# A residual kernel with a generated right-hand matrix: first chunks of W and base loaded singly, base chunk 0 cast ahead of W chunk 1, one product of zeros for five, two base units moved up

## The chip, the cores and the metric

The kernel runs on one core of one Trainium2 chip. A core has five engines, each with its own queue of instructions: TensorE (PE in the profile; its weight loads are PEld), VectorE (DVE), ScalarE (ACT), GpSimd (POOL) and SyncE (SP, which here only issues transfers). The metric is the device time of one execution in microseconds; lower is better.

## The reference

x has 8 batches of 1024 rows of 512. A second input, cond (8 x 512), makes for each batch a 512 x 512 matrix of rank 8, which is added to a fixed matrix `base`. Then each batch gets a second, modulated product with a fixed matrix W. Cut to what matters:

```python
ae = layernorm(cond, ln_g, ln_b)                       # 8 x 512
h = gelu(ae @ w1 + b1)                                 # 8 x 512
xw = h @ w2 + b2                                       # 8 x 8192, w2 is 16 MB
x_a, x_b = split(xw, 2); each reshaped to (8, 512, 8)
layer = base[None] + einsum('bdr,bkr->bdk', x_a, x_b)  # 8 x 512 x 512
x = x + (x + einsum('btc,bco->bto', x, layer))
ys = cond * 512 ** -0.5
d = rsqrt((ys * ys) @ (W * W) + 1e-8)                  # 8 x 512
x = x + einsum('bsi,io->bso', x * ys[:, None], W) * d[:, None]
```

## The kernel before

All matrices are held in four chunks of 128 rows (k = 0 to 3), one after the other along the free dimension of a tile of 128 partitions. For each batch b the kernel makes one matrix, P_b = (2I + base + rank term) · (I + diag(ys_b) W diag(d_b)), so that the output is one product per batch, x_b · P_b. Every product of 32-bit floats is done as three products of `fp32r` tiles: each operand is split into a head (rounded; names with h) and a rest (names with l), and head·head, head·rest and rest·head are added up in PSUM. One such triple of 128 x 128 by 128 x 512 products, for one chunk k and one block c of output rows, is called a base unit when its left operand is base.

The program first sets up (to about 80 us) and then runs the main loop over 8 batches and 8 row tiles (`po`, line 799), in which TensorE is the only limit. In the setup almost everything is in an order written out by hand (`InOrder`, `keep_in_program_order`): each engine runs its instructions in the order of the program's text.

The setup's steps that the change and the prediction touch, with the names of the profile:

- **Loads** (lines 86 to 92), all issued by SP in this order: `sm` (small vectors, identity), `cnd` (in tile `scr`), W chunks 0 and 1 (`w_sb`), base chunks 0 and 1 (`b_raw`), W chunks 2 and 3, base chunks 2 and 3, then `w1` (the page calls it `w_sb<-in_w` too), then the sixteen 1 MB tiles of `w2` (`w`) as buffers come free, with `consts`, `condrows`, `b2rows` and `base` between them.
- **Zeros** (lines 102 to 111): twelve products of a tile of zeros (`warm`), started at once, and five more (`keep_warm(5)`, line 256) between the transposes `pa` of the normalised cond (`ae`) and the first base products. Their results are not used.
- **Right operands of the first batch**: `round_yw(k)` (ScalarE, W chunk times ys, head `nh`), `rest_yw(k)` (VectorE, rest `nl`). d is not known yet and is multiplied in later.
- **Left operands**: `twice_i(k)` (VectorE, adds 2I to the diagonal block), `round_b(k)` (ScalarE, head `bh`; for chunk 0, VectorE does the first 128 columns and ScalarE the other 384), `rest_b(k)` (VectorE, rest `bl`).
- **First base products** (`pg`, line 257): all four head·head products of chunk 0, then the four head·rest (`nl`), then the four rest·head (`bl`). Then chunk 1 (`first_base`), mixed with the row products for d (`pq_v`, which reads the squares of W, `wsq`) and for h (`pq_z`, which reads `w1`).
- **`w2` groups** (`w2_group`, line 387): each issues the load of a `w2` tile into one of nine big buffers and runs that tile's four products (`px`, eight instructions in the profile). `Fill.units(n)` puts n base units of batches 1 to 3 (`pq`) between them. `rank_t` is a chain of steps on xw's second half: `by`, its transposes `pb`, the product `pt_t`, and the stacked rows `ps_t`; each `next(steps)` runs one step.

The part of lines 725 to 742 that orders this:

```python
w2_group()
w2_group()
fill.units(6)
w2_group()
steps = rank_t()
next(steps)          # by
w2_group()
next(steps)          # its rest
fill.units(4)
w2_group()
next(steps)          # pb, byT
w2_group()
fill.units(2)
fill.round(2, 1)
next(steps)          # pt_t
```

Of the kernel before, what the change touches and what calls it, by code (L numbers as in the profile page):

```python
# [14 lines left out]
P = 128  # L15
NB = 8
NT = 1024
D = 512
# [12 lines left out]
def cond_resid_kernel(ctx: ExitStack, tc: tile.TileContext, small, cond, condrows, consts,  # L31
# [12 lines left out]
    def mm(*args, **kw):  # L44
        tc.keep_in_program_order(nc.tensor.matmul(*args, **kw))  # L45

    def turn(*args):
        tc.keep_in_program_order(nc.tensor.transpose(*args))
# [36 lines left out]
    cnd, ae, xab, drow = scr[:NB, 0, :], scr[:NB, 1, :], scr[:, 2, :], scr[:, 3, :]  # L85
    sy.dma_start(sm, small)
    sy.dma_start(cnd, cond)
    for at in (slice(0, 2), slice(2, 4)):
        sy.dma_start(w_sb[:, at, :], weight[:, at, :])
        sy.dma_start(b_raw[:, at, :], baseT[:, at, :])  # L90
    w1_sb = big_tile("w1_sb")
# [14 lines left out]
    def keep_warm(count):  # L106
        for _ in range(count):
            mm(warm.rearrange("p (a c) -> p a c", c=P), zero,
               zero.unsqueeze(1).to_broadcast([P, D // P, P]), start=True, stop=True)
# [29 lines left out]
    def round_yw(k):  # L139

        se.mul(n0[k][0], w_sb[:, k, :], ysT[:, k, 0:1])
# [6 lines left out]
    def twice_i(k):  # L148
        blk = b_raw[:, k, k * P:(k + 1) * P]
        ve.scalar_tensor_tensor(blk, ident, 2.0, blk, ALU.mult, ALU.add)  # L150

    def round_b(k, lo=0, hi=D, by=se.copy):
        (by(bh[:, k, lo:hi], b_raw[:, k, lo:hi]))
# [29 lines left out]
    rstd = sp.tile([NB, 1], F32, name="rstd")  # L183
    ve.tensor_mul(rstd, r, t)
    ve.tensor_scalar(ae, cnd, mv[:, 0:1], rstd, ALU.subtract, ALU.mult)
    round_yw(1)
    twice_i(0)
    round_b(0, 0, P, ve.tensor_copy)
    round_b(0, P, D)
    twice_i(1)  # L190
    round_b(1)
    rest_yw(0)
# [60 lines left out]
    pa = misc.tile([P, KC, NB], F32, tag="misc", name="pa")  # L253
    for k in range(KC):
        turn(pa[:, k, :], ae[:, k * P:(k + 1) * P], ident[:NB, :NB])
    keep_warm(5)
    for i, (s, m) in enumerate(((bh, n0[0][0]), (bh, n0[0][1]), (bl, n0[0][0]))):
        for c in range(KC):
            mm(pg[c], s[:, 0, c * P:(c + 1) * P], m, start=(i == 0), stop=False)
# [127 lines left out]
    def w2_group():  # L387
        h, r, k = todo.pop(0)
        t = big_tile(f"w2_{h}_{r}_{k}")
        sy.dma_start(t, w2[h, r, k])  # L390
        if len(todo) == 15:
            sy.dma_start(cst, consts)
        if len(todo) == 8:
            sy.dma_start(crow, condrows)
            sy.dma_start(b2r, b2rows)
        if len(todo) == 6:
            b_nat.append(big_tile("b_nat"))
            sy.dma_start(b_nat[0], base)
        for j in range(4):
            mm(px[h][32 * j:32 * j + 32, :], hT[:, k, r, :], t[:, j, :],  # L400
               start=(r == 0 and k == 0), stop=(r == 1 and k == KC - 1))
# [296 lines left out]
    fill = Fill()  # L698
# [31 lines left out]
    next(steps)  # L730
    w2_group()
    next(steps)
    fill.units(4)
    w2_group()
    next(steps)
    w2_group()
    fill.units(2)
    fill.round(2, 1)
    next(steps)
    fill.finish(2, 1)  # L740
# [191 lines left out]
```

## Time and profile before

| | |
|---|---|
| median of 3 runs | 305.32 us (305.03 to 305.65) |
| the profiled execution | 305.47 us, span of its instructions 303.7 us |
| granted TensorE clock, mean | 0.998 |
| TensorE busy | 298.0 us (98% of the span) |
| VectorE / ScalarE busy | 176.4 / 145.9 us |
| read from HBM, written | 40.35 MB, 16.79 MB |

Times in the profile's views are microseconds from the span's start. A line of a timeline gives start, duration, engine, source line, operation, tile written <- tiles read, shapes, and how often; in brackets stands the engine's idle time just before it and what ended that. The source line is often that of a helper (L45 is `mm`, L62 the in-order wrapper), so instructions are told apart by their tiles. A line of the chain of waits gives start, duration and what the end of the program was then waiting on.

### The profile page before, as it was taken

The numbers are of one execution on the slowest core, as the hardware profiler recorded it, in microseconds if no ns is written. First come the engines' busy times: TensorE is split into PE (matmuls) and PEld (weight loads), VectorE is DVE, ScalarE is ACT, GpSimd is POOL, SyncE is SP. The second block draws the span as 40 slices with busy tenths as digits, with TensorE's granted clock in tenths as the row PEclk, the third lists the DMA queues.
The fourth block names the chain that finished last, engine by engine and source line by source line (L and its number), as shares of the span: only waits on it lengthen the run. The fifth ranks groups of instructions, "written<-read, shape, count | busy, mean of one in ns | idle before, by whom it ended". The sixth has DMA issues, their size and how long they took to land.

```text
span 303.7 us, 3551 instructions
## 1 busy us (share of the span) xinstructions
PE 298.0 (98%) x1369; PEld 227.9 (75%) x1369; DVE 176.4 (58%) x262; ACT 145.9 (48%) x212; POOL 5.2 (2%) x14
## 2 busy tenths in 40 slices
PE   8999999999999999999999999999999999999995
PEld 3655565466888888888888888888888888888884
DVE  4779830979678479977456478981266543600000
ACT  4756132256476564355664454743645546621221
POOL 0011000001000000100000000000000000000000
PEclk9999999999999999999999999999999999999999
DMA  6999999642319636631651134354151545322222
GB/s 204 409 427 419 410 421 419 220 188 69 138 69 343 242 124 226 228 120 69 207 193 52 69 108 171 97 162 192 69 207 69 190 178 212 148 106 104 96 76 105
DMA packets 15952, 57.37 MB, mean 189 GB/s; under 512 B 1840, under 2 KB 2352, under 8 KB 11584
## 3 DMA queue, kind: packets, MB, share of 16 engines
q1 hardware_dynamic: 6064, 38.78, 34.5%
q10 hardware_dynamic: 9360, 16.78, 14.7%
q0 software_dynamic: 512, 1.59, 1.6%
q8 instruction: 10, 0.16, 0.2%
q14 instruction: 6, 0.05, 0.1%
HBM read 40.35 MB, written 16.79 MB: 188 GB/s over the span
## 4 chain that ended last, share of the span: by engine, by line
PE 88%; DVE 5%; DMA 4%; ACT 2%; issue 0%; ACTq 0%
PE po L45 57%; PE pp L45 13%; PE pq L45 7%; DMA w<-in_w 4%; PE px L45 3%; PE warm L45 2%; PE pg L45 2%; DVE n L62 2%; PE pr L45 2%; PE pt_t L45 1%; ACT work L62 1%; DVE scr L62 0%; PE ps_t L45 0%; DVE q L62 0%; PE pq_v L45 0%
## 5 line engine op out<-in xcount | busy, mean ns | idle before, releaser
L45 PE MATMUL po<-ph,xs 128*128 128x512 f32 (+1 forms) x520 | 164.2, 386 | 0.0
L45 PEld LDWEIGHTS po<-ph,xs 128*128 128x128 f32 x520 | 97.1, 188 | 19.8
L45 PE MATMUL po<-pl,xs 128*128 128x512 f32 (+1 forms) x260 | 100.3, 386 | 0.0
L62 ACT COPY o<-po 128x512 f32<-128x512 f32 (+1 forms) x65 | 37.8, 581 | 87.0 <-PE po L45 86.8
L45 PEld LDWEIGHTS po<-pl,xs 128*128 128x128 f32 x260 | 48.8, 188 | 9.9
L62 DVE TENSOR_TENSOR xs<-x,xs 128x1024 fp32r<-128x1024 f32 x32 | 38.7, 1221 | 20.5 <-ACT xs L62 20.5
L62 ACT CAST xs<-x 128x1024 fp32r<-128x1024 f32 x32 | 33.0, 1050 | 4.0 <-DMA x<-in_x 2.3
L62 DVE TENSOR_TENSOR nl_p<-n,nh_p 128x1024 fp32r<-128x1024 f32 x14 | 17.1, 1220 | 20.0 <-ACT nh_p L62 20.0
L62 DVE TENSOR_TENSOR pl<-q,ph 128x1024 fp32r<-128x1024 f32 x16 | 19.4, 1220 | 7.3 <-ACT ph L62 7.3
L62 DVE TENSOR_TENSOR q<-pr,q 128x512 f32<-128x512 f32 x24 | 15.8, 685 | 7.9 <-PE pr L45 7.8
L45 PE MATMUL pq<-nh,bh 128*128 128x512 f32 x48 | 19.8, 412 | 0.0
L45 PE MATMUL pq<-nl,bh 128*128 128x512 f32 x48 | 19.1, 398 | 0.1
L45 PE MATMUL pq<-nh,bl 128*128 128x512 f32 x48 | 19.0, 395 | 0.0
L62 ACT CAST ph<-q 128x1024 fp32r<-128x1024 f32 x16 | 16.6, 1051 | 3.9 <-DVE q L62 3.7
L62 DVE SCALAR_TENSOR_TENSOR n<-w_sb,ysT,d 128x512 f32<-128x512 f32 x24 | 17.8, 745 | 0.8 <-DMA d<-d_out 0.8
L62 ACT COPY q<-pp 128x512 f32<-128x512 f32 x20 | 11.7, 587 | 13.3 <-PE pp L45 13.3
L45 PE MATMUL px<-w,hT 128*32 128x512 f32 x128 | 16.0, 601 | 0.4 <-DMA w<-in_w 0.4
L62 ACT CAST nh_p<-n 128x1024 fp32r<-128x1024 f32 x14 | 14.7, 1052 | 2.5 <-PE pp L45 2.4
L45 PEld LDWEIGHTS pq<-nh,bh 128*128 128x128 f32 x48 | 9.0, 188 | 8.4 <-issue 5.0
L45 PE MATMUL pp<-nh_p,sh 128*128 128x512 f32 x32 | 12.4, 389 | 0.0
L45 PE MATMUL pp<-nl_p,sh 128*128 128x512 f32 x32 | 12.4, 389 | 0.0
L45 PE MATMUL pp<-nh_p,sl 128*128 128x512 f32 x32 | 12.4, 389 | 0.0
(135 smaller groups left out, 272.9 us busy)
## 6 DMA issues: line engine op xcount, KB each, us to landing
w<-in_w SPq DMA_DIRECT2D x16, 1024.0 KB, 11.1
x<-in_x SPq DMA_DIRECT2D x16, 1024.0 KB, 5.2
out<-o ACTq DMA_DIRECT2D x63, 256.0 KB, 2.0
d<-d_out POOLq DMA_DIRECT2D x6, 256.0 KB, 3.9
w_sb<-in_weight SPq DMA_DIRECT2D x2, 512.0 KB, 5.4
b_raw<-in_baseT SPq DMA_DIRECT2D x2, 512.0 KB, 6.2
w_sb<-in_w SPq DMA_DIRECT2D x1, 1024.0 KB, 9.6
b_nat<-in_base SPq DMA_DIRECT2D x1, 1024.0 KB, 9.5
```

The costliest lines, as they stand in the source:

```text
L45: tc.keep_in_program_order(nc.tensor.matmul(*args, **kw))
L62: return lambda *a, **kw: pin(f(*a, **kw)) if InOrder.on else f(*a, **kw)
```

## The change

It changes four places. The first four chunk loads become W chunk 0, base chunk 0, W chunk 1, base chunk 1, of 256 KB each; chunks 2 and 3 stay together. In ScalarE's order `round_b(0)` (its 384 columns) changes places with `round_yw(1)`. After `pa` one product of zeros runs instead of five. Two base units that stood after the second `w2` group behind `fill.units(4)` now run before both groups.

```diff
-    for at in (slice(0, 2), slice(2, 4)):
+    for at in (slice(0, 1), slice(1, 2), slice(2, 4)):
         sy.dma_start(w_sb[:, at, :], weight[:, at, :])
         sy.dma_start(b_raw[:, at, :], baseT[:, at, :])
...
-    round_yw(1)
+    round_b(0, P, D)
     twice_i(0)
     round_b(0, 0, P, ve.tensor_copy)
-    round_b(0, P, D)
+    round_yw(1)
     twice_i(1)
     round_b(1)
     rest_yw(0)
...
-    keep_warm(5)
+    keep_warm(1)
...
     next(steps)
-    fill.units(4)
+    fill.units(6)
     w2_group()
     next(steps)
     w2_group()
-    fill.units(2)
     fill.round(2, 1)
     next(steps)
```

## The prediction

> **What bounds the kernel now.** I read the page first (engine shares, the DMA row), then the chain of waits in order of time, the timeline of the first ten microseconds, the DMA view of the first 16, and TensorE's timeline around the one wait for a `w2` tile.
>
> ```profile
> PE 298.0 (98%) x1369; PEld 227.9 (75%) x1369; DVE 176.4 (58%) x262; ACT 145.9 (48%) x212; POOL 5.2 (2%) x14
> ...
> DMA  6999999642319636631651134354151545322222
> ```
>
> TensorE runs its products in program order and is busy almost throughout, so time can only come from the places where it waits or does idle work. The DMA row says that for the first 50 us or so (slices of 7.6 us) the transfer engines are full as well: there, a `w2` tile lands when the bytes ahead of it have passed. The chain of waits shows both:
>
> ```profile
> 0.99 5.00 PE warm L45 x12
> 5.99 0.34 PE pa L48 x4
> 6.33 1.19 PE warm L45 x5
> 7.51 4.38 PE pg L45 x18
> ...
> 34.91 1.90 PE px L45 x16
> 36.81 0.02 issue
> 36.83 11.16 DMA w<-in_w
> 47.99 0.04 issue
> 48.03 1.06 PE px L45 x8
> ```
>
> Two places, then: nothing useful runs on TensorE before 7.5, and at 48.03 it has stood waiting for a tile that landed at 36.83 + 11.16 = 47.99. The front in the timeline (start, duration, engine; all engines):
>
> ```profile
> 5.45 1.33 ACT L62 ACTIVATE nh<-w_sb,ysT 128x512 fp32r<-128x512 f32 x2 [1.44 <-DMA w_sb<-in_weight]
> 6.78 0.29 DVE L62 SCALAR_TENSOR_TENSOR b_raw<-sm,b_raw 128x128 f32<-128x128 f32 x1 [1.30 <-DMA b_raw<-in_baseT]
> 7.10 0.23 DVE L62 CAST bh<-b_raw 128x128 fp32r<-128x128 f32 x1
> 7.25 0.28 DVE L62 SCALAR_TENSOR_TENSOR b_raw<-sm,b_raw 128x128 f32<-128x128 f32 x1
> 7.44 0.76 PEld L45 LDWEIGHTS pg<-nh,bh 128*128 128x128 f32 x4 [0.42 <-ACT bh L62]
> 7.45 0.74 DVE L62 SCALAR_TENSOR_TENSOR nl<-w_sb,ysT,nh 128x512 fp32r<-128x512 f32 x1
> ```
>
> The first base product waits for `bh` chunk 0, that for base's first half, which landed at 6.75. VectorE's `twice_i(1)` (7.25) and then `nl` chunk 0 (7.45) follow at once only because chunk 1 came in the same transfer.
>
> **The change, part by part.**
>
> *Four loads of 256 KB for two of 512 KB.* The loads pass in turn through full engines; the DMA view, in slices of 0.4 us, gives the rate:
>
> ```profile
> GB/s 0 0 0 0 124 138 123 195 317 195 184 297 451 410 420 369 246 215 195 277 328 338 471 410 471 440 430 410 430 471 410 389 492 369 393 441 426 382 448 451
> ```
>
> From 2.4 the slices to 4.8 add up to 525 KB, W's first half at some 230 GB/s; the next three hold base's first half at 427 GB/s; then 521 KB to 8.0, W's second half at 260. W is read slowly, base fast, both with rows of the same size. By bytes, W chunk 0 (first quarter) has passed at 3.7, base chunk 0 at 4.8, W chunk 1 at 5.4, base chunk 1 at 6.0. Before, the half that passed at 4.8 landed at 5.42 and that of 6.0 at 6.75. So the chunks land at about 4.4, 5.4, 6.1 and 6.75. Rows of 2 KB instead of 4 KB cost a little: the 256 KB of `condrows`, with 2 KB rows, landed 0.66 after the load ahead of it, while 256 KB of a 1 MB load take 2.50 / 4 = 0.62; four such pieces add 0.15. Base chunk 1: 6.9; everything behind it, 0.15 later. Two more issues on SP cost 0.35 to 0.43 each, and push W's rest, `w1` and the first `w2` loads back by 0.85; W's rest is then issued at about 3.4 and wanted at 6.2, `w1` at 4.4 and wanted at 9.7, so SP stays ahead. Base's half landed 1.33 after W's, all of it bytes at 512 KB and 427 GB/s, so what a load costs besides its bytes is hidden behind the load ahead of it, and I charge nothing for the two more loads themselves. A rule of the Trainium skill speaks against this part: "DMA: Bandwidth & Descriptors", Anatomy of one DMA, gives each DMA a fixed 2.0 us besides its bytes (a fit for loads issued from GpSimd). If that were paid in turn, two more loads would cost 4 us, base chunk 1 would land at 10.75, and the sum below would end near 308.3; I go by the row.
>
> *Base chunk 0 cast ahead of W chunk 1.* ScalarE: `nh` 0 from 4.4 to 5.1, then its 384 columns of `bh` 0 (0.51) from 5.45 to 5.95. Behind it in the queue `nh` 1 (0.71) waits for W chunk 1, 6.1 to 6.8; its first reader, the products of chunk 1, comes after 9.7. With the old order, `nh` 1 would hold `bh` 0 up to 6.8, so the move is needed. VectorE ends `ae` at 5.47, then `twice_i(0)` and its 128 columns by 6.02 (before: 0.55 from landing to 7.33).
>
> *One product of zeros for five.* Four at 0.23 are 0.92 of TensorE. They were cover: the fifth began at 7.14, and the first base product at 7.47. Now `pa` ends at 6.3, one product ends at about 6.5, and the first base product starts at 6.55, 0.92 earlier; `bh` 0 is ready 0.4 before that. Where the cover is gone, a later chunk costs 1:1.
>
> *What is late next.* The four `nh`·`bh` products take until 7.55 (before 7.47 to 8.47: 1.00). The next need `nl` 0, and VectorE reaches that only after `twice_i(1)`, which now waits for base chunk 1 alone; `nl` 0, `bl` 0, `nl` 1, `bl` 1 all stand behind it. Landing 6.9, + 0.03, + 0.20 to the next start, + 0.74, + 0.05 to TensorE: 7.92. So TensorE stands for 0.37 and goes on at 7.92 against 8.47: 0.55 earlier. `bl` 0 ends at 8.5 and is wanted at 8.9. W chunk 2's square still waits for its landing (9.34 + 0.15) and the squares end at 10.7; the product that reads them starts at 11.82 − 0.55 = 11.27. `bh` 2 (11.64 before, + 0.15) is read at 14.6 or later; `w1` (13.06 + 0.15) at 14.3. From 14 to 36 every wait of TensorE (`pd` at 22.05, `nl` at 27.24) hangs on its own earlier products through VectorE and ScalarE and moves along. **0.55** stays. Bounds: with W read as fast as base, chunk 1 lands 0.8 to 1 earlier and TensorE never stops: 0.92. With W's slowness a price per row rather than per byte, the next part but one.
>
> *Two base units moved up.* Around the wait:
>
> ```profile
> 45.95 1.06 PE L45 MATMUL px<-w,hT 128*32 128x512 f32 x8
> 46.95 0.65 PE L48 MATMUL pb<-sm,work 128*128 128x128 f32 x4
> 48.03 1.06 PE L45 MATMUL px<-w,hT 128*32 128x512 f32 x8 [0.43 <-DMA w<-in_w]
> 49.03 0.50 PE L45 MATMUL pq<-nh,bh 128*128 128x512 f32 x1
> ```
>
> Without a wait this group would start 0.20 after the last `pb` (as `pq_z` does after `pt_v`, 14.64 to 14.85), at 47.53: the wait is 0.50. Two units are 6 products of 0.23 = 1.39. They now stand ahead of the group: 47.53 − 0.55 + 1.39 = 48.37, and the tile lands at 47.99 + 0.15 = 48.14. The wait goes whole, **0.50**, with 0.23 to spare; without the move, the 0.55 of the front would be lost at this place. `pt_t` follows the group directly: `pb` starts 1.0 after the group before, `byT` is done 1.28 later (46.95 to 48.23 before), `pt_t` is reached 2.6 after that group's start: 0.3 of slack. The moved units read `nh`/`nl` of base 2, done at 38.7. The later `w2` tiles keep their slack: the last was issued at 57.48, when the group that ended at 57.35 let go of its buffer, and landed 4.8 later, 0.6 before use; that issue moves with TensorE.
>
> Sum: 0.55 + 0.50 = 1.05. The profiled execution took 305.47 (span 303.7 and 1.77 around it), 0.15 above the median and inside the runs' 305.03 to 305.65. 305.47 − 1.05 = 304.4; from the median it would be 304.3.
>
> **The rivals.**
>
> *Only the second half arrives (no change).* Something at the front (the slow W, a semaphore between chunk and cast) eats the 0.55, for example W's excess, 2.3 − 1.2 = 1.1 us per half, counted per row: chunk 1 of base at 8.0, TensorE at 9.0, 0.5 late, and the 0.50 gained back at 48: 305.4. If just half of it is so, 304.9. For: W alone is slow. Against: base has the same rows and isn't, and the 2 KB rows of `condrows` weren't.
>
> *A thin row of W costs what a thick one did (slower).* Place: W chunks 0 and 1 ahead of base chunk 1. Each then takes W's 2.3 for half the bytes: base chunk 1 lands at 6.75 + 2.3 = 9.05, TensorE goes on at 10.07, 1.60 late, with 0.50 back: 306.6. It decides against the change once base chunk 1 lands after 7.95.
>
> *The clock falls where the zeros are gone (slower).* Row: the zero products start 0.43 apart until 5.2 and 0.23 apart after 6.3, so full speed took some 4.6 us of work; falling back would cost 4.6 / 0.43 = 11 products at 0.20 more, 2.1: 306.5. The longest stand that the trace shows at full clock is 0.58 (21.25 to 22.05); mine is 0.37. "TensorE: Matmul & The Clock Gate", Part 1, puts the window of inactivity at about 3.4 us, by which the clock stays.
>
> **How the numbers follow.** Forecast 0.70 (303.9 to 304.7), no change by the first rival 0.20, thin rows 0.07, clock 0.03. About 0.2%, 0.6 us, is what a measurement of this kernel can tell from no change: faster means under 304.7. Of the forecast a little falls short of that, of the first rival a little passes it: 0.71, 0.20, 0.09. The range runs from the front's best, 0.92 + 0.50 off the median, 303.9, to the first rival's 305.4, rounded out by 0.1 below, and leaves the slower rivals out.
>
> **What would show it.** Right: first base product at about 6.5; `nh` 0 at 4.4; a stand of some 0.4 ahead of `pg<-nl,bh`, which starts near 7.9; `pq_v` near 11.3; no DMA wait at 48, `pt_t` near 49.5 instead of 50.53. Wrong: base chunk 1 landing after 7.5; TensorE standing at the squares (`pq_v`) or at the moved group; a spacing of 0.43 after 7.

## The result and the profile after

The changed kernel took 308.55 us (median of 12 executions, 305.55 to 310.98) against 305.29 for the kernel before: 1.0084 times its time, 95% interval 1.0055 to 1.0114 (the ratio leaves out the two longest executions). The forecast was 304.4, range 303.8 to 305.4, so the time lies outside it, on the side of the slower rivals. The executions differ from each other far more than before, and the mean granted TensorE clock goes with the time: 1.0 in two of them (305.6 and 305.8), 0.993 or 0.994 in seven (307.6 to 309.2) and 0.987 in three (309.6 to 311.0). In the 94 executions of the kernel before that were timed beside the experiments it was 0.997 or more, but for one at 0.995.

The profiled execution is one of the two with a whole clock: 305.55, span 303.6. Its page:

```profile
PE 297.1 (98%) x1365; PEld 227.4 (75%) x1365; DVE 176.5 (58%) x262; ACT 145.9 (48%) x212; POOL 5.1 (2%) x14
...
DMA  6999999652319737631651134255151455422222
```

TensorE is 0.9 us less busy (four products of zeros), and the span is the same: where it no longer runs zeros, it waits. The timeline of the front (start, duration, engine; in brackets the idle time before and what ended it):

```profile
5.70 0.29 DVE L62 SCALAR_TENSOR_TENSOR b_raw<-sm,b_raw 128x128 f32<-128x128 f32 x1
6.40 1.17 PE L45 MATMUL pg<-nh,bh 128*128 128x512 f32 x4
8.25 0.29 DVE L62 SCALAR_TENSOR_TENSOR b_raw<-sm,b_raw 128x128 f32<-128x128 f32 x1 [1.99 <-DMA b_raw<-in_baseT]
8.46 0.74 DVE L62 SCALAR_TENSOR_TENSOR nl<-w_sb,ysT,nh 128x512 fp32r<-128x512 f32 x1
9.25 1.20 PE L45 MATMUL pg<-nl,bh 128*128 128x512 f32 x4 [1.69 <-DVE nl L62]
```

The first base product starts at 6.40 (7.47 before). But VectorE, with `nl` 0 queued behind `twice_i(1)`, waits for base chunk 1 until 8.25, and TensorE stands until 9.25, where before it had gone on at 8.47. A stretch in which TensorE has no product to run is called a stand here; counted from the start of one product to the next, less a product's 0.23, this one is 1.85. The chain of waits says the same in two lines:

```profile
2.93 5.29 DMA b_raw<-in_baseT
...
9.25 3.53 PE pg L45 x14
```

Further on, at the place of the old wait for a `w2` tile, TensorE's timeline has none:

```profile
48.12 1.06 PE L45 MATMUL px<-w,hT 128*32 128x512 f32 x8
49.11 0.66 PE L48 MATMUL pb<-sm,work 128*128 128x128 f32 x4
49.70 1.06 PE L45 MATMUL px<-w,hT 128*32 128x512 f32 x8
50.70 0.50 PE L45 MATMUL pt_t<-wh,work 128*128 128x512 f32 x1
```

`pt_t` starts at 50.70 (50.53 before), although `pq_v` started 0.89 later than before (12.71 against 11.82). So in this execution, with a whole clock, all but 0.17 of the late front is paid back by 50.70, and the time is that of before. What makes the median slower is not in this profile.

### The profile page after: what moved, and what is told of

The parts are those of the page before. It is cut to its first block, busy times and chain, and to the rows that moved or that the text cites. A ratio compares the mean times of both kernels' runs of the same rounds, so it can differ in the third digit from the quotient of the medians.

```text
span 303.6 us, 3547 instructions
## 1 busy us (share of the span) xinstructions
PE 297.1 (98%) x1365; PEld 227.4 (75%) x1365; DVE 176.5 (58%) x262; ACT 145.9 (48%) x212; POOL 5.1 (2%) x14
## 4 chain that ended last, share of the span: by engine, by line
PE 89%; DVE 5%; DMA 2%; ACT 2%; SPq 1%; issue 1%; ACTq 0%; DVEq 0%
PE po L45 57%; PE pp L45 13%; PE pq L45 9%; PE px L45 4%; DVE n L62 2%; DMA b_raw<-in_baseT 2%; PE pg L45 2%; PE pr L45 2%; PE pt_t L45 1%; SPq L62 1%; ACT work L62 1%; DVE nl L62 0%; DVE scr L62 0%; PE ps_t L45 0%; DVE q L62 0%
```

## The experiments

Theory A: base chunk 1 lands late, TensorE stands 1.85 us, and the stand makes the clock fall. Theory B: the long executions have still later landings, the clock only follows. Theory C: it is the four missing zeros that close the clock. Each kernel was timed beside the kernel before: `fill_stand`, `loads_back`, `rest_first` and `units_only` beside 29 executions of it (median 305.39), `no_zeros`, `cast_only`, `rest_first_no_units` and `base_rest_first` beside another 29 (305.53), the three `joint` ones beside 23 (305.66), `mixed` beside 13 (305.25). A ratio is that to the kernel before, with its 95% interval.

**fill_stand.** 

> The changed kernel with eight products of zeros put between the four head-head and the four head-rest products of chunk 0, where its profile shows TensorE standing 1.85 us. Theory A (base chunk 1 lands near 8.2, TensorE stands 1.85 us, and in most executions this stand makes the clock fall for one or two windows, which costs 2 to 4 us): with the stand filled, nearly every execution at clock 0.998 to 1.0 and 305.4 to 306.0 us. Theory B (the long executions are long because chunk 1 lands later still, and the clock only follows): still 307 to 310 us with scatter, and clock below 0.995. Theory C (it is the four zeros missing ahead of the first base product that close the clock): as B.

```diff
     for i, (s, m) in enumerate(((bh, n0[0][0]), (bh, n0[0][1]), (bl, n0[0][0]))):
+        if i == 1:
+            keep_warm(8)
```

306.49 (305.70 to 306.73), ratio 1.0031 (1.0019 to 1.0043), all five executions with a clock of 0.998 or more, where the changed kernel had two of twelve. So it is the stand that makes the clock fall, and filling it with idle work takes some 2 us off the changed kernel's median: against B and C. The time was above what A gave (305.4 to 306.0). In the profile base chunk 1 landed at 9.25, and after the eight zeros TensorE still stood 0.8 until `nl` 0 was ready, so the zeros held nothing up; `pt_t` started at 51.78, 1.25 later than before. So the remaining 1.1 over before goes, in this profile at least, with the late landing itself.

**no_zeros.** 

> The changed kernel without the last product of zeros, so that TensorE idles 0.2 us more ahead of the first base product. One look at the profile. Theory A (stands close the clock in most executions): with chance 0.8 the granted clock falls to half after the stand near 7.5 to 9, products there 0.43 apart instead of 0.23 for one window; 307 to 311 us, mean clock 0.994 or 0.987. Theory B: the clock is whole and the time long all the same.

```diff
-    keep_warm(1)
+    keep_warm(0)
```

One execution, 307.79, clock 0.994: its profile holds the fallen clock. TensorE's timeline, then two views by stretch (start:end, length, busy us of PE, PEld, DVE, ACT, POOL; then the granted clock, the DMA share and GB/s), of this kernel and of the changed one:

```profile
7.02 1.17 PE L45 MATMUL pg<-nh,bh 128*128 128x512 f32 x4 [1.00 <-DVE bh L62]
10.08 1.27 PE L45 MATMUL pg<-nl,bh 128*128 128x512 f32 x4 [1.89 <-DVE nl L62]
11.14 1.91 PE L45 MATMUL pg<-nh,bl 128*128 128x512 f32 x4
```

```profile
7.60:11.00 3.40, 1.51 (x7) 0.94 (x6) 1.93 (x4) 1.73 (x5) 0.00 (x0) 1.00 1.01 363
11.10:14.40 3.30, 3.30 (x9) 2.58 (x8) 3.27 (x10) 2.87 (x5) 0.00 (x0) 0.50 0.99 419
14.50:17.90 3.40, 3.40 (x21) 1.87 (x19) 0.45 (x1) 1.11 (x2) 0.74 (x2) 1.00 1.01 421
```

```profile
5.00:8.40 3.40, 2.57 (x13) 1.19 (x10) 1.26 (x5) 1.91 (x3) 0.00 (x0) 1.00 1.02 306
8.40:11.80 3.40, 2.55 (x11) 2.11 (x12) 3.37 (x9) 3.23 (x6) 0.00 (x0) 1.00 1.03 423
```

The trace's clock record has full speed from 4.22 to 11.05, half from 11.05 to 14.46, full again after: steps of 3.41 us. Four products of `nh`·`bl` take 1.91 instead of 1.10. In the step before the fall TensorE was busy for 1.51 of 3.4. In the changed kernel's profile the steps begin at 5.00 and 8.41, and the stand of 7.40 to 9.25 is cut in two by one: 2.57 and 2.55 of 3.4 busy, and the clock stays. One fallen step costs half of 3.4, 1.7 us, and makes a mean clock of 0.994; two would make 0.989 (one execution of `joint_thin` has that). The 0.987 of three executions of the changed kernel would be two such steps and a piece of one behind the last product, as in the profile before, whose 0.998 comes from half speed after 302.50; no profile holds such an execution. Where the steps lie differs between executions (the first full-speed step began at 3.64 to 6.92 in the profiles). That this is why the same kernel falls in one execution and not in the next is likely, but no pair of profiles of one kernel shows it.

**loads_back.** 

> The changed kernel with the first loads as two of 512 KB again; cast order, one product of zeros and moved units stay. TensorE is then without work from about 6.5 to 7.5 (1.0 us) where the zeros were, and goes on as before the change; the moved units save the 0.5 us wait. Theory A: the thin loads are the cause; chunk 1 lands at 6.75, the stand is 1.0 instead of 1.85 us; about 305.0 us, clock mostly whole. Theory C: without the four zeros the clock falls in most executions, 307 to 309 us. If the clock falls in part of the executions, the length of the stand decides the share.

```diff
-    for at in (slice(0, 1), slice(1, 2), slice(2, 4)):
+    for at in (slice(0, 2), slice(2, 4)):
```

305.14 (304.92 to 306.62), ratio 1.0002 (0.9990 to 1.0015); clock 0.994 in 2 of 11. Base's first half landed at 6.82 and TensorE stood 1.35 ahead of the first base product. As A has it: with the old loads no late chunk and few falls; against C, which had most executions falling. With the zeros gone the stand ahead of the first base product is still long enough for a fall now and then.

**rest_first.** 

> The changed kernel with VectorE's rest of W and of base, chunk 0, ahead of its step that waits for base chunk 1. Theory A: TensorE goes through the twelve products of chunk 0 from 6.4 to about 9.2 without a stand, chunk 1 is ready at about 9.2 to 9.4, the first product that waits is that of the squares (about 11.3 against 11.82 before); 304.4 to 305.0 us, clock at 0.998 or more in nearly all executions, scatter under 1 us. Theory B: gains the stand too, but executions of 307 us and more stay where chunk 1 lands late. Theory C: clock still falls, 306 to 309 us.

```diff
-    twice_i(1)
-    round_b(1)
     rest_yw(0)
     rest_b(0)
+    twice_i(1)
+    round_b(1)
     rest_yw(1)
```

305.01 (304.17 to 306.93), clock 0.998 or more in all 12, ratio 0.9998 (0.9982 to 1.0014). The stand after the first four products is gone, and with it the falls. The scatter stays, against the forecast of under 1 us: two executions took 306.50 and 306.93 with clocks of 1.0 and 0.998. Chunk 1 still lands late (8.26 in this profile), which is the likely reason; no profile of a long execution shows it.

```profile
6.99 1.18 PE L45 MATMUL pg<-nh,bh 128*128 128x512 f32 x4 [0.43 <-DVE bh L62]
8.01 1.10 PE L45 MATMUL pg<-nl,bh 128*128 128x512 f32 x4
8.94 1.08 PE L45 MATMUL pg<-nh,bl 128*128 128x512 f32 x4
```

**units_only.** 

> The kernel before with only the two base units moved up. The wait of 0.5 us at 48.03 goes: 304.8 us, clock 0.998. If what the move gives is taken back later: 305.3 us.

```diff
-    fill.units(4)
+    fill.units(6)
     w2_group()
     next(steps)
     w2_group()
-    fill.units(2)
```

305.37, ratio 1.0000 (0.9990 to 1.0011): no gain; the 304.8 missed. In its profile base's first half landed at 7.30 and the first base product started at 8.02, so the front was 0.55 later than in the profile that the sum was made from. TensorE did not wait at 48, and `pt_t` started at 50.51 (50.53 before): what the move gave, the front had lost.

**cast_only.** 

> The kernel before with ScalarE's cast of base chunk 0 ahead of its step on W chunk 1, nothing else. Both chunks of W and of base come in one load each there, the cast waits for base in either order, and the step on W chunk 1 has 2 us to spare: 305.4 us, as before. Its profile also shows once more when base's first half lands (6.75 in the profile before, 7.30 in that of units_only) and whether TensorE waits near 48.

```diff
-    round_yw(1)
+    round_b(0, P, D)
     twice_i(0)
     round_b(0, 0, P, ve.tensor_copy)
-    round_b(0, P, D)
+    round_yw(1)
```

305.38, ratio 1.0003 (0.9994 to 1.0012), as expected. Base's first half landed at 7.13, the first base product started 0.39 later than in the profile before, and at 48 TensorE did not wait at all: the tile had landed at 47.75.

```profile
47.29 0.65 PE L48 MATMUL pb<-sm,work 128*128 128x128 f32 x4
47.87 1.06 PE L45 MATMUL px<-w,hT 128*32 128x512 f32 x8
```

The two units are in their old place here. So the wait of 0.50 is there in one profile with the old order and not in the other.

**rest_first_no_units.** 

> The changed kernel with chunk 0's rests ahead of VectorE's wait for base chunk 1 (as in rest_first), but the two base units back in their old place. Theory: an early front and the moved units give one gain, not two: without the move, TensorE waits at the second w2 group for the tile that lands near 48, whatever the front gained; median 305.3 to 305.7 us, no execution below 304.8, where rest_first had 305.0 and reached 304.2. Rival: the move is worth nothing by itself even then; 305.0 us as rest_first.

 The edit is rest_first's with the two base units in their old place.

305.49 (305.07 to 307.25), ratio 1.0003 (0.9988 to 1.0018), and no execution below 305.07, where rest_first reached 304.17. In its profile the group waits some 0.15 for its tile, landed at 48.21. That is as expected if the early front and the moved units are one gain: six of rest_first's twelve executions were under 305.0, none of these. But the gap between the two medians, 0.48, is not clear of noise (the intervals of the two ratios overlap), and this profile has a late front (chunk 1 landed at 9.13, `pq_v` started at 12.01), so it does not show an early front being lost at 48.

**base_rest_first.** 

> The changed kernel with base chunks 2 and 3 loaded ahead of W chunks 2 and 3. In the runs so far packets take 1.5 to 2 times their usual time from 3.0 to 4.4 and from 6.0 to 8.4, where W's first rows and W's second half pass. Theory W (W's second half is slow to read, and slows the last engines of base chunk 1 that it runs beside): the slow stretch moves to about 7.2 to 9.5, base chunk 1 lands at 7.0 to 7.4 in all engines, TensorE's stand ahead of the head-rest products falls from 1.85 to about 0.5 us, and the clock stays whole in most executions: 305.0 to 306.0 us (the squares of W come about 1 us later). Theory T (the stretch from 6.0 to 8.4 is slow whatever is loaded): base chunk 1 still lands at 8.0 or later, the stand stays at 1.7 us or more, 307 to 310 us.

```diff
+    sy.dma_start(b_raw[:, 2:4, :], baseT[:, 2:4, :])
+    sy.dma_start(w_sb[:, 2:4, :], weight[:, 2:4, :])
```

The two loads stand in place of the loop's for chunks 2 and 3. 305.25 (304.99 to 306.86), ratio 0.9996 (0.9980 to 1.0011), clock 0.994 in one of 12. In its profile base chunk 1 landed at 8.03 in its last engine, and the stand was 1.32. The time is what theory W gave (305.0 to 306.0), the landing what theory T gave (8.0 or later): the stretches of slow packets were spread thinner, from 3 to 8. Whether W or the time makes them stays open. But the four thin loads are still there, and the median is back at that of the kernel before: thin rows alone do not make 308.55. What passes behind base chunk 1 counts too.

**joint, joint_thin.** 

> The changed kernel with W and base in one array, chunk by chunk: its first two loads bring W chunk 0 with base chunk 0, and W chunk 1 with base chunk 1, 512 KB each in rows of 4 KB (the bytes come in the changed kernel's order, in the loads and rows of the kernel before). Chunks 2 and 3 as before. Theory P (in the slow stretches a packet waits about 0.3 us whatever its size, so rows of 2 KB double the price and a few engines fall 1 to 2 us behind): base chunk 1 lands at 6.7 to 7.3, the stand ahead of the head-rest products is 0.3 to 0.8 us, the clock whole in nearly all executions; the sum of the prediction comes out, 304.3 to 305.0 us. Theory O (the order, W and base in turn, is what makes base chunk 1 late): lands at 8 or later, 307 to 310 us as the changed kernel.

 

> As joint with the same number of loads in the same order, but W and base apart in memory, so that the first two loads read rows of 2 KB. Theory P: as late as with four thin loads, base chunk 1 in its last engine at 8.0 to 9.3, stand 1.3 us or more, 306 to 309 us with clocks of 0.994 in part of the executions. Theory N (it is the number of loads, not the rows): base chunk 1 lands at 6.7 to 7.3 and the time is that of joint.

```diff
-        sy.dma_start(w_sb[:, at, :], weight[:, at, :])
-        sy.dma_start(b_raw[:, at, :], baseT[:, at, :])
+    for i in range(KC):    # joint: wb_in holds W0 b0 W1 b1 W2 W3 b2 b3
+        sy.dma_start(wb[:, 2 * i:2 * i + 2, :], wb_in[:, 2 * i:2 * i + 2, :])
...
+    # joint_thin: wb_in holds W0 W1 W2 W3 b0 b1 b2 b3
+    for i, at in enumerate((slice(0, 5, 4), slice(1, 6, 4), slice(2, 4), slice(6, 8))):
+        sy.dma_start(wb[:, 2 * i:2 * i + 2, :], wb_in[:, at, :])
```

Both kernels read W and base from one array; the comments tell the order of its chunks. Same number, order and size of loads; what differs in the edit is the rows of the first two, 4 KB against 2 KB. To make room, both have two output buffers instead of four and `dst` in another tile, so their times compare with each other better than with the rest: 305.61 (305.23 to 305.83, clock 0.998 or more in all 12), and 307.53 (306.60 to 308.75, clock 0.989 to 0.994 in four of six). The second pair landed at 7.69 in `joint` (half of the engines by 7.05) and at 8.82 in `joint_thin` (7.82). TensorE's lines, `joint`'s first:

```profile
8.73 0.50 PE L45 MATMUL pg<-nl,bh 128*128 128x512 f32 x1 [0.15 <-DVE nl L62]
9.86 1.65 PE L45 MATMUL pg<-nl,bh 128*128 128x512 f32 x3 [0.43 <-DVE nl L62]
```

The executions of the two do not overlap, so with the same number of loads in the same order the rows make the difference. It has two parts: SP takes 0.60 and 0.65 to issue the two loads with thin rows (0.35 and 0.43 in `joint`), so that the second goes out 0.33 later, and the rest of the 1.13 comes in the transfer. The landings are of one profile each. Of theory P, 8.82 is as forecast, 7.69 is later than its 6.7 to 7.3, and its time for `joint` (304.3 to 305.0) missed: the first pair landed at 6.41, so the first base product started at 7.21.

**joint_rest_first.** 

> As joint, with chunk 0's rests ahead of VectorE's wait for base chunk 1 (as in rest_first). Theory P: no stand at all after the first base product, which starts at 6.6 to 6.9; 304.0 to 304.7 us with less scatter than rest_first (304.2 to 306.9), and faster than both kernels. Theory O: as rest_first, 305.0 us with its scatter.

 The edit is joint's with rest_first's.

305.23 (305.01 to 306.99), ratio 0.9997 (0.9981 to 1.0012), clock 0.994 in 2 of 12: theory P's 304.0 to 304.7 missed. The pairs landed at 6.61 and 7.86, the first base product started at 7.41 after a stand of 1.2.

**mixed.** 

> A version put together from the runs so far: W chunk 0 and base chunk 0 in a load each (rows of 2 KB), W chunk 1 with base chunk 1 in one load with rows of 4 KB, then W and base chunks 2 and 3; chunk 0's rests ahead of VectorE's wait for base chunk 1; two products of zeros; the two base units moved up; four output buffers as in the kernel before (from the seventh output on they lie in base's space, which is free by then). Theory P: base chunk 0 lands at 5.7 to 6.3 and the first base product starts at 6.5 to 7.0 (joint_rest_first: 7.41); the pair of chunks 1 lands at 7.5 to 8.0 in all engines, so nothing stands until the squares; clock whole; 304.2 to 304.9 us with less scatter than rest_first. Theory O (the landings scatter as they do whatever the rows): 305.0 us and a scatter of 2 us, as rest_first.

 Its loads, in `joint`'s array:

```diff
+    for at in (slice(0, 1), slice(1, 2), slice(2, 4), slice(4, 6), slice(6, 8)):
+        sy.dma_start(wb[:, at, :], wb_in[:, at, :])
...
-    keep_warm(1)
+    keep_warm(2)
```

304.55 (304.21 to 305.01), clock 0.999 or more in all nine: 0.9977 of the kernel before (0.9967 to 0.9987), and faster than both kernels. Base chunk 0 landed at 6.01 and the pair of chunks 1 at 7.30. TensorE's timeline:

```profile
6.79 1.28 PE L45 MATMUL pg<-nh,bh 128*128 128x512 f32 x4
7.90 1.10 PE L45 MATMUL pg<-nl,bh 128*128 128x512 f32 x4
...
11.27 1.07 PE L45 MATMUL pq_v<-wsq,ysq 128*32 128x512 f32 x8
...
49.54 0.50 PE L45 MATMUL pt_t<-wh,work 128*128 128x512 f32 x1
```

## Why the prediction was wrong

**The step that failed** is "By bytes … the chunks land at about 4.4, 5.4, 6.1 and 6.75", with 0.15 for thin rows: base chunk 1 at 6.9. It landed at 8.22, and between 8.03 and 9.25 in the six profiles with four thin loads. The trace's landing records, engine by engine, show how the step went wrong: half of the 16 transfer engines had finished base chunk 1 by 6.84, as forecast, but VectorE waits for the last one, and three came at 8.0 to 8.2. A rate in GB/s averages over the engines and can't show that. The first three chunks were nearer (5.00, 5.68, 6.36); being 0.68 apart, they also show that two more loads did not cost 2 us each in turn.

By the prediction's own path the 1.32 us of later landing are enough for the two executions with a whole clock: 304.4 and 1.32 are 305.7, and they took 305.6 and 305.8. The rest of the median, 2.9 us, comes with the fallen clock, and perhaps with still later landings in those executions, which no profile of the changed kernel shows (9.05 in `no_zeros`).

The row used for thin rows, `condrows`, could not show the late engines: the 0.66 is the distance of two last landings, 36.12 and 36.78, and the engine before the last had finished `condrows` at 35.45. On an engine that is behind for both loads the distance is only that engine's time for its share. Its packets also ran in a quiet stretch (28 to 36 of the profile before, one packet in some 600 over 1.5 times its usual time), and those at issue beside slow ones. The records of single packets support a price per packet: those that were slow took on average some 0.25 us longer than the usual 0.084 with 2 KB in the changed kernel, and some 0.18 longer than 0.159 with 4 KB before. That this is why a few engines fall behind was not tested; that rows of 2 KB land later than rows of 4 KB in the same order, `joint` and `joint_thin` show. Two readings were off without weight: 525 KB from 2.4 to 4.8 are 219 GB/s and not 230, and 512 KB at 427 GB/s take 1.23 us, so that 0.1 of the 1.33 between the landings was not bytes.

**The thin-row rival** had the idea, a price per row, and the point at which the gain is gone, "once base chunk 1 lands after 7.95". It had the wrong place: it let W chunks 0 and 1 come late, and W chunk 1 landed at 6.36 (6.1 forecast); the delay came behind that, in the last engines of base chunk 1. It was given 0.07.

**The clock rival** was the larger part: of the 3.2 us between the medians (308.55 and, beside `fill_stand`, 305.39), the filled stand took 2.1 away (306.49), which go with the clock; the other 1.1 are the landing's. It was given 0.03 because the longest stand in the trace was 0.58 and the forecast stand 0.37; the second follows from the landing that failed, and measured 1.85. It was also bound to the missing zeros, and `loads_back`, which lacks them too, fell in 2 of 11 only. It was priced at 2.1, from a first warm-up of 4.6 us; a fallen step lasts 3.41 and costs 1.7, so the sum was near for a reason that did not hold.

The clock changed in steps of 3.41 us, and it fell after a step with 1.51 us busy in `no_zeros`, and after one with 2.14 in `joint_thin`. The Trainium skill, "TensorE: Matmul & The Clock Gate", Part 1, has a free-running window of about 3.4 us; the steps agree. The same part has the clock fall after at least one idle window; by these two steps less than that is enough.

**What held.** The first base product at 6.40 (6.55 forecast); `nh` 0 limited by its chunk; no wait at 48. Everything behind `pq_v` moved with TensorE. `mixed`, where chunk 1 lands in time, comes out where the sum did: `pq_v` at 11.27 (11.27 forecast), `pt_t` at 49.54 (49.5), the profiled execution 304.39 (304.4). That is partly luck: it is another kernel (rests moved, two zeros, chunks 1 in one load), its first base product starts at 6.79 and not at 6.55, and it has no stand where 0.37 was forecast. Its median is 0.70 below that of the kernel before, not 1.05.

**Mis-sized**: the 0.50 at 48 is worth nothing by itself (`units_only`). It was read from one execution with an early front; with the later front of `cast_only` it is not there. It and the 0.55 of the front are not two gains in every execution: the move gained nothing where the front was late (`units_only`). That an early front's gain is lost at 48 without the move is likely by `rest_first_no_units`, and not shown.

## What to carry to other kernels

A load was as late here as its slowest transfer engine: when an in-order engine waits for a transfer, read the last engine's landing over several profiles, not a mean rate. Cover taken from TensorE has to be judged by the longest stand that a late transfer can make: with a stand of 1.85 us in the profile the clock fell in 10 of 12 executions (changed kernel), with 1.44 in 4 of 6 (`joint_thin`), with 1.2 to 1.35 in one or two of 11 or 12 (`base_rest_first`, `loads_back`, `joint_rest_first`), with 0.93 or less in none (`joint`, `rest_first`, `mixed`); each fallen step cost another 1.7 us. Put work that needs no new data ahead of the wait. A gain read at a wait that one execution shows should be looked for in a second one before it is added to another.

## What was not expected of the hardware

- The granted clock changes in steps of 3.41 us and falls to half for one step after one in which TensorE was busy 1.51 (`no_zeros`) or 2.14 us (`joint_thin`); it held after 2.13 (`no_zeros`, the step before) and 2.17 (`loads_back`). Behind the last products it fell after 1.15 (profile before, step from 299.06) and held after 1.65 (`loads_back`, from 298.24, and `no_zeros`, from 301.16). So the busy time of one step does not decide by itself; what does stays open. Where the steps lie differs from execution to execution.
- In the first 8 us, packets take up to 1 us instead of 0.08 (2 KB) or 0.16 (4 KB) in the profiles before and after, and up to 1.95 in `joint`, in two stretches (about 3 to 4.4 and 6 to 8.4 in most profiles). From 12 to 28 hardly any take over 1.5 times as long; from 28 to 36 some do again in half of the profiles (34 in the changed kernel, one in the kernel before). The cause stays open.
- The same first loads land up to 0.6 us apart in different executions (four kernels whose first loads are those of the kernel before: base's first half at 6.75, 6.82, 7.13 and 7.30).
